# A two-layer graph network: the first adjacency's row sums from TensorE to ScalarE, one cast reordered, one load on another queue

## The chip, the cores and the metric

The kernel runs on one core of one Trainium2 chip. A core has five engines that run side by side, each with its own instruction queue in order: TensorE (PE in the profile, with its weight loads as PEld), VectorE (DVE), ScalarE (ACT), GpSimd (POOL) and SyncE (SP, which issues DMAs here). Sixteen DMA engines move data between DRAM and the on-chip memory. An engine's queue waits at an instruction until the semaphores it needs have been raised by other engines or by DMAs. The metric is device time in microseconds (us) of one whole execution; the time of a kernel is the median of its runs.

## The reference

There are 16 graphs of N = 1024 nodes with C = 128 features. `adj` (16 x 1024 x 1024) holds zeros and ones and is symmetric with a filled diagonal; the kernel's exact path relies on its entries being short numbers. Cut to what matters:

```python
# layer 0: four rounds of a gated network, all graphs apart
h = relu(layernorm(x))
for i in range(4):
    hw = einsum('bnc,cd->bnd', h, weight[i])
    m  = einsum('bjn,bjd->bnd', adj, hw)
    h  = gru_cell(m, h, w_ih[i], w_hh[i], b_ih[i], b_hh[i])
x = x + h * mask
# layer 1: four convolutions, normed over all graphs after each
h = relu(layernorm(x))
for i in range(4):
    h = relu(einsum('bnm,bmc->bnc', adj, h @ W[i]) + b[i])
    mu, var = mean and variance of h over graphs and nodes
    h = gamma[i] * (h - mu) * rsqrt(var + 1e-5) + beta[i]
return x + h
```

## The kernel before

Each product with an adjacency is done in two parts. The left factor is split into a high part, rounded to a format that TensorE multiplies fast (`hw[0]`, a cast on ACT), and the low rest (`hw[1]`, a subtraction on DVE), and both are multiplied with the adjacency's rows (`aggregate_rows`, L520 to L530, 32 matmuls of 128x512 per graph and round). The first part of the kernel runs the gated network, the second the four convolutions.

**The gated network** runs as two streams, `sa` with the even graphs and `sb` with the odd ones. A step (`half_step`, L1105) does the gates of one stream (24 matmuls at L1000, and sigmoids, a tanh and elementwise work on ACT and DVE) and then the sums with the adjacency of the other (L524), while ACT and DVE finish the gates. After a sum ACT copies its two halves out of the accumulators (`m`, L961), and the next step's gates read them. A number `clock[0]` counts the steps: the first two streams' first rounds are steps 3 and 4, step 5 has its gates at 79 us in the trace and a step takes some 17.6 us. In this part the order of every engine is the order of the program text (`manual_schedule` with all five engines, L1170). Work that belongs to no stream's own round is put into a step by `at(step, place, what)`; `due(place)` emits it, and the places of a step are, in order, "ins", "start", "beside0", "looks", "mid", "beside1", "outs", "gap" and "end".

Around the change, this is in the steps:

- `next_load` (L808, "beside0") loads the x of the stream's next graph into one of four buffers of the tag "x" (`flat`, L389). It is issued from ACT's queue. `next_sums` (L811, "gap" of the same step) takes its layer-norm sums on DVE (L664), `next_factors` (L814, "gap" of the next step) the root on ACT (L668) and two small DVE operations. There are 14 such loads, in pairs in neighbouring steps, one pair in eight steps.
- The norm of the layer's output is spread over steps in the same way (`plan`, L825): `store_xmid` (L752, "mid", a DMA from POOL), `blocks` (L680, ACT), `store_ymid` (L755, "mid", from POOL).
- "mid" is emitted by `mids` (L1098): POOL first copies one column of the stream's new h (`pace`, L1101), and so waits for DVE's last operation on it (L1044), then stores.
- The transposer (`transposes`, L618) casts each adjacency row to bf16 on POOL (L615) into one of two buffers `half`, has SP issue a transposing DMA, and at last stores the turned adjacency `adjT_d` for the convolutions.
- In the fourth round of a stream SP loads the next graph's adjacency rows into `stage`, POOL rounds them into `row` tiles (L577), and ACT or DVE looks whether their low bits are zero (`glance`, L580 to L586, an ACTIVATE with an accumulated sum and an output `junk` that nobody reads; `look`, L606, on DVE).

For the first two graphs the rows are in place from the start: `sa.rows` are graph 0's eight tiles of 128x1024, read by the sums of graph 0's four rounds (the last three in steps 3, 5 and 7) and by the transposer, and overwritten with graph 2's from step 8 on.

**The convolutions.** `load_adjT` (L1318) loads eight rows of the turned adjacency in bf16 (`packed`, `block`) and casts them (`wide`, ACT for every third, DVE for the rest) into twelve `row` buffers. In the first convolution the weights are applied after the sums (`first_weights`, L1389); `first_split` (L1381) loads the stored y on POOL's queue, casts it to the high part `chw` on ACT (L1385) and subtracts on DVE (L1386). A `chw` tile shares its buffer with the gated network's `ghw` of the same parity, so the cast can run only after the last matmul that reads that `ghw`. Graph 0 also gets `row_sums` (L1417): 16 matmuls with a tile of ones (`ones_r`, cast at L1463) add up graph 0's rows into two accumulators (`pt_deg`), so that every partition holds every node's row sum, and two ACT copies (L1426) put them into `degree`, which lies in the first 1024 columns of the gated network's `w_mT`. `raw_weights` (L1406) reads `degree` in convolutions 1 to 3, where graph 0's sum is taken before the norm's shift is known and the shift times the row sum is added afterwards (L1413).

The last gates of `sb` (b = 15), the turns of the last h's (`pt_x`, L735) and `last_tail` (L757) overlap with the first convolution. In this part only PE, POOL and SP keep the program's order, and only within the block at L1298 to L1303; a planner with modelled times orders the rest. `tc.issue_after(ins)` is a constraint for it: an instruction of the block that runs on the engine of `ins` comes after `ins` in that engine's queue. `last_m` (L961) is a stream's latest copy of a sum; after the gated network `sb.last_m` is that of graph 15's last round.

Of the kernel before, what the change touches and what calls it, by code (L numbers as in the profile page):

```python
# [8 lines left out]
F32 = mybir.dt.float32  # L9
F32R = mybir.dt.float32r  # L10
BF16 = mybir.dt.bfloat16
U16 = mybir.dt.uint16
I32 = mybir.dt.int32
AF = mybir.ActivationFunctionType
ALU = mybir.AluOpType
AX = mybir.AxisListType
P = 128
HALF = 512
# [323 lines left out]
def exact_path(  # L342
# [21 lines left out]
    nc = tc.nc  # L364
    B, N, C = x.shape
    L = g_weight.shape[0]
    NB = N // P
    NH = N // HALF
# [3 lines left out]
    const = ctx.enter_context(tc.tile_pool(name="const", bufs=1))  # L372
    small = ctx.enter_context(tc.tile_pool(name="small", bufs=2))
    dram = ctx.enter_context(tc.tile_pool(name="dram", bufs=1, space=bass.MemoryType.DRAM))
# [7 lines left out]
    def tmp(name):  # L382
        return ps_t.tile([P, HALF], F32, tag="tmp", name=name)

    adjT_d = [dram.tile([NB, P, N], BF16, tag=f"adjT{b}", name=f"adjT_d{b}") for b in range(B)]
    xmid_d = [dram.tile([N, C], F32, tag=f"xmid{b}", name=f"xmid_d{b}") for b in range(B)]
    ymid_d = [dram.tile([P, N], F32, tag=f"ymid{b}", name=f"ymid_d{b}") for b in range(B)]

    def flat(name):  # L389
        return keep.tile([P, NB, C], F32, tag="x", name=name, bufs=4)  # L390
# [10 lines left out]
    def hw_tiles(b, name):  # L401
        return [keep.tile([P, N], F32R, tag=f"hw{b % 2}{s}", name=f"{name}_{s}") for s in range(2)]
# [5 lines left out]
    nc.vector.memset(eps_t, EPS)  # L408
    ones = const.tile([P, 1], F32, tag="ones", name="ones")
    nc.vector.memset(ones, 1.0)  # L410
    low = const.tile([P, (B + 2) * NB], F32, tag="low", name="low")
    nc.vector.memset(low, 0.0)

# [52 lines left out]
    def turn_hh(i):  # L466

        pt = tmp(f"pt_whh{i}")
        for g in range(3):
            nc.tensor.transpose(pt[:, g * P : (g + 1) * P], wns["hh", i][:, g, :], ident)  # L470
        nc.scalar.copy(w_hhT[:, i, :], pt[:, : 3 * P])

    def turn_ih(prep, w_g, i):

        pt = tmp(f"pt_wih{i}")
        for g in range(3):
            nc.tensor.transpose(pt[:, g * P : (g + 1) * P], wns["ih", i][:, g, :], ident)
        nc.tensor.transpose(pt[:, 3 * P :], w_g[:, i, :], ident)
        both = prep.tile([P, 4 * C], F32, tag="w_both", name=f"w_both{i}", bufs=1)
        nc.scalar.copy(both, pt)  # L480
        turned[i] = both[:, 3 * C :], both[:, : 3 * C]

    def join_layer(i):
        w_gT, w_ihT = turned[i]
        pw = tmp(f"pt_wm{i}")
        nc.tensor.matmul(pw[:, : 3 * P], w_gT, w_ihT, start=True, stop=True)
        nc.scalar.copy(w_mT[:, i, :], pw[:, : 3 * P])
# [29 lines left out]
    def aggregate(pm, hw, rows, g):  # L517
        aggregate_rows(pm, hw, rows, range(g * BH, (g + 1) * BH))
# [14 lines left out]
    with ExitStack() as st:  # L533
        work = st.enter_context(tc.tile_pool(name="work", bufs=2))
        rawd = st.enter_context(tc.tile_pool(name="rawd", bufs=2, space=bass.MemoryType.DRAM))

        def load_x(b, eng):
            xt = flat(f"x{b}")
            eng.dma_start(xt, x[b].rearrange("(k p) c -> p k c", p=P))
            return xt  # L540
# [39 lines left out]
        def glance(b, stage, js):  # L580

            junk = work.tile([P, N], BF16, tag="junk", name=f"junk{b}_{js[0]}", bufs=1)
            for j in js:
                lows = stage[j % 4].bitcast(U16).rearrange("p (n t) -> p n t", t=2)[:, :, 0]
                k = b * NB + j
                nc.scalar.activation(junk, lows, AF.Copy, accum_out=low[:, k : k + 1])  # L586

        def exchange_out(t, name, d=None):
            if d is None:
                d = rawd.tile([P, HALF], F32, tag="cross", name=f"cross_{name}", bufs=8)  # L590
            nc.sync.dma_start(d, t)
            return d
# [25 lines left out]
        def transposes(batches):  # L618

            for b, rows in batches:  # L620
                adjT = turned_tile(f"adjT{b}")
                ahead = transpose_rows(b, rows[0], 0, adjT)
                for j in range(NB):
                    go = ahead
                    if j + 1 < NB:
                        ahead = transpose_rows(b, rows[j + 1], j + 1, adjT)
                    go()
                    yield j
                nc.gpsimd.dma_start(adjT_d[b].rearrange("k p n -> p k n"), adjT)
                yield NB  # L630
# [139 lines left out]
        class Stream:  # L770
# [35 lines left out]
                norm_blocks(self.xt, self.y, self.norm, ks)  # L806

            def next_load(self):  # L808
                self.next_x = load_x(self.b + 2, nc.scalar)

            def next_sums(self):  # L811
                self.next_norm = norm_stats(self.next_x, f"in{self.b + 2}")
# [256 lines left out]
        def at(n, place, go):  # L1069
            agenda.setdefault((n, place), []).append(go)  # L1070
# [5 lines left out]
        def first_step(one, two, gated, halfway):  # L1076

            feed.next_step()
            if one is sa:
                feed.jobs = transposes([(s.b, s.rows) for s in (sa, sb)])  # L1080
            one.split_step()
            feed.some(2)
            two.gate_step(0)
            two.half_away(0)
            if feed.full or (clock[0], "mid") in agenda:
                mids(two)
            feed.some(1)
            two.gate_step(1)
            two.half_away(1)
            gated()  # L1090
            one.agg_step(0)
            halfway()
            feed.some(NB if one is sa else 1)
            one.agg_step(1)
            two.finish()
            clock[0] += 1

        def mids(two):  # L1098

            pace = small.tile([P, 1], F32, tag="pace", name=f"pace{clock[0]}")  # L1100
            nc.gpsimd.tensor_copy(pace, two.new[:, :1])  # L1101
            feed.store()
            due("mid")
# [63 lines left out]
        sa, sb = Stream(0), Stream(1)  # L1167
        every = {getattr(mybir.EngineType, e) for e in ("PE", "DVE", "Activation", "Pool", "SP")}
        prep = st.enter_context(tc.tile_pool(name="prep", bufs=1))
        with tc.manual_schedule(engines=every):  # L1170
# [111 lines left out]
            def ahead(i):  # L1282
                join_layer(i)
                if i + 1 < L:
                    turn_hh(i + 1)

            sa.plan(0)
            sb.plan(1)
            first_step(sa, sb, looks, lambda: ahead(1))
            first_step(sb, sa, lambda: turn_ih(prep, w_g, 2), lambda: ahead(2))  # L1290
            written[0] = False
# [23 lines left out]
    work = ctx.enter_context(tc.tile_pool(name="work2", bufs=2))  # L1315
# [53 lines left out]
    def banks(b, i):  # L1369
        return [acc(t, f"pc{b}_{i}_{t}") for t in (("m0", "m1") if b % 2 == 0 else ("g_r", "g_z"))]  # L1370

    def conv_done(b, i, pm, stats, halfway=None):
        for hf in range(NH):
            dst = feat[b][:, hf * HALF : (hf + 1) * HALF]
            last = nc.scalar.activation(dst, pm[hf], AF.Relu, bias=cvec(0, i))  # L1375
            nc.vector.bn_stats(stats[:, b * NH + hf, :], dst)  # L1376
            if halfway and hf == 0:
                sums = halfway()
        return sums if halfway else last

    def first_split(b):  # L1381
        yt = flat(f"y{b}").rearrange("p k c -> p (k c)")
        nc.gpsimd.dma_start(yt, ymid_d[b])
        hw = hw_tiles(b, f"chw{b}_0")
        nc.scalar.copy(hw[0], yt)  # L1385
        nc.vector.tensor_sub(hw[1], yt, hw[0].bitcast(F32))  # L1386
        return hw

# [17 lines left out]
    def raw_weights(i, pm, aff, stats):  # L1406
# [6 lines left out]
            nc.vector.scalar_tensor_tensor(mt[:, cols], degree[:, cols], aff[1], mt[:, cols], ALU.mult, ALU.add)  # L1413
            nc.tensor.matmul(pc[hf], w_c[:, i, :], mt[:, cols], start=True, stop=True)
        conv_done(0, i, pc, stats)

    def row_sums(rows):  # L1417

        pd = [tmp(f"pt_deg{hf}") for hf in range(NH)]
        for j in range(NB):  # L1420
            for hf in range(NH):
                nc.tensor.matmul(
                    pd[hf], ones_r, rows[j][:, hf * HALF : (hf + 1) * HALF], start=(j == 0), stop=(j == NB - 1)
                )
        for hf in range(NH):
            nc.scalar.copy(degree[:, hf * HALF : (hf + 1) * HALF], pd[hf])  # L1426

    xo = []

# [29 lines left out]
            for n0, n in pieces(k):  # L1459
                nc.gpsimd.dma_start(xo_piece(k, n0, n), by_node(xmid_d[k], n0, n))  # L1460

    ones_r = work.tile([P, P], F32R, tag="ones_r", name="ones_r", bufs=1)
    nc.vector.tensor_copy(ones_r, ones.to_broadcast([P, P]))  # L1463
    degree = w_mT.rearrange("p l c -> p (l c)")[:, :N]

    stats = small.tile([P, B * NH, 6], F32, tag="bn_st", name="stats0")
    hw, waiting = first_split(0), None
    for b in range(B):
        rows = load_adjT(b, 0)
        hw_next = first_split(b + 1) if b + 1 < B else None  # L1470
        pm = banks(b, 0)
        aggregate(pm, hw, rows, 0)
        if waiting:
            last = first_weights(*waiting, stats)
            if b == 1:
                with tc.issue_after(last.ins):
                    sb.rest()
        if b == B - 1:
            hw_next = raw_split(1)
        aggregate(pm, hw, rows, 1)  # L1480
        if b == 0:
            row_sums(rows)
        hw, waiting = hw_next, (b, pm)


# [1 line left out]
    for i in range(1, L):  # L1487
        rows, pm0, hw0 = load_adjT(0, i), banks(0, i), hw
# [6 lines left out]
        hw = conv_hw(1, i, conv_input(1, i, aff, 2))  # L1495
        aggregate_rows(pm0, hw0, rows, range(6, NB))
        for b in range(1, B):
            rows = load_adjT(b, i)
# [18 lines left out]
            hw = hw_next  # L1517
# [9 lines left out]
    for b in range(B):  # L1527
# [3 lines left out]
        for n0, n in pieces(b):  # L1531
# [5 lines left out]
            tag = turns[count % len(turns)]  # L1537
# [60 lines left out]
```

## Time and profile before

| | |
|---|---|
| time, median of 3 runs | 1770.71 us |
| the three runs | 1769.65, 1772.32, 1770.71 us |
| the profiled execution | 1769.17 us |
| span of its instructions | 1767.4 us |
| granted TensorE clock | 0.999 |

| engine | busy us | instructions |
|---|---|---|
| PE | 1752.3 | 6734 |
| DVE | 1289.3 | 2310 |
| ACT | 1112.0 | 1713 |
| POOL | 362.9 | 401 |

| stretch us | PE busy us | DVE | ACT | POOL | DMA share |
|---|---|---|---|---|---|
| 60 to 1110, gated network | 1049.86 | 809.06 | 626.28 | 312.63 | 0.71 |
| 1110 to 1136, its last rounds | 25.70 | 17.61 | 12.52 | 1.10 | 0.92 |
| 1136 to 1156, last gates | 20.00 | 16.48 | 11.05 | 3.62 | 0.68 |
| 1156 to 1169, row sums of graph 0 in it | 12.98 | 9.01 | 10.83 | 1.45 | 0.86 |
| 1169 to 1290, rest of the first convolution | 121.00 | 78.19 | 86.49 | 12.30 | 0.85 |
| 1290 to 1436, the second | 145.66 | 94.74 | 105.16 | 0.00 | 0.65 |

A line of a timeline is: start (us from the span's start), duration, engine, line of the kernel, operation, what it writes <- what it reads, shape, how many in a row; in brackets the idle time of the engine before it and what ended that. "ACTq" is ACT's queue issuing a DMA. Names are the program's with numbers left out. A busy PE can still be slow, since matmuls overlap and their ends are modelled; so starts are compared. The profiled execution is one run, and the difference between its own time and its span lies around the instructions.

### The profile page before, as it was taken

The page shows a single profiled execution, that of the slowest core. Times are in us where ns is not written, and L with a number is a line of the kernel's source. Part 1 is how long each engine was busy: PE and PEld are TensorE (multiplying, and loading weights), DVE is VectorE, ACT ScalarE, POOL GpSimd, SP SyncE. Part 2 cuts the span into 40 slices and gives each one's busy share as a digit, 9 for nine tenths or more (in the row PEclk, how much of TensorE's full clock was granted, in tenths as well). Part 3 has the DMA queues.
Part 4 walks back from the last instruction along what each step waited for, and adds up shares of the span by engine and source line. Part 5 has one row for each costly group of instructions (what it writes and reads, how often), then busy time and mean ns, then how long its engine had stood idle before and what let it go on. Part 6 is the DMA issues. An engine that isn't in the chain of part 4 may idle for free. (4 is left out here: it accounts for less than half of the span.)

```text
span 1767.4 us, 22310 instructions
## 1 busy us (share of the span) xinstructions
PE 1752.3 (99%) x6734; PEld 1192.7 (67%) x6734; DVE 1289.3 (73%) x2310; ACT 1112.0 (63%) x1713; POOL 362.9 (21%) x401
## 2 busy tenths in 40 slices
PE   9999999999999999999999999999999999999997
PEld 5565656565656565656565656577778888888886
DVE  7677877877877887877887786766666666666665
ACT  5356556557556556655655664487677767767765
POOL 4214213322332331321422323110100000000011
PEclk9999999999999999999999999999999999999999
DMA  7458568577686676776866857887866665757667
GB/s 261 138 169 280 166 180 301 158 223 248 196 214 221 221 212 216 238 197 200 270 185 178 305 137 228 287 290 289 292 220 215 234 243 210 256 202 258 230 220 270
DMA packets 376160, 400.14 MB, mean 226 GB/s; under 512 B 158188, under 2 KB 254224, under 8 KB 376032
## 3 DMA queue, kind: packets, MB, share of 16 engines
q1 hardware_dynamic: 342736, 323.59, 58.0%
q0 software_dynamic: 18208, 67.46, 10.2%
q10 hardware_dynamic: 15088, 7.60, 1.5%
q8 instruction: 54, 0.88, 0.2%
q14 instruction: 74, 0.61, 0.1%
HBM read 267.47 MB, written 97.52 MB: 207 GB/s over the span
## 5 line engine op out<-in xcount | busy, mean ns | idle before, releaser
L524 PE MATMUL pm<-row,ghw 128*128 128x512 f32 x2048 | 503.9, 403 | 0.5 <-POOL row L563 0.3
L524 PEld LDWEIGHTS pm<-row,ghw 128*128 128x128 f32 x2048 | 383.6, 188 | 107.1 <-issue 25.6
L524 PE MATMUL pc_m<-wide,chw 128*128 128x512 f32 x1024 | 245.2, 395 | 0.0
L615 POOL CAST half<-row 128x1024 bf16<-128x1024 f32 x128 | 143.7, 1133 | 402.3 <-DMA adjT<-half 387.4
L524 PEld LDWEIGHTS pc_m<-wide,chw 128*128 128x128 f32 x1024 | 190.4, 188 | 41.9 <-issue 3.8
L961 ACT COPY m<-pm 128x512 f32<-128x512 f32 x128 | 68.7, 588 | 195.4 <-PE pm L524 195.4
L1023 ACT ACTIVATE r<-r,vecs 128x512 f32<-128x512 f32 x128 | 92.2, 721 | 152.8 <-DVE r L1020 148.8
L524 PE MATMUL pc_g_r<-wide,chw 128*128 128x512 f32 x464 | 186.9, 403 | 0.3 <-ACT chw L501 0.3
L1019 DVE SCALAR_TENSOR_TENSOR r<-g_hn,vecs,r 128x512 f32<-128x512 f32 x128 | 93.3, 729 | 128.5 <-ACT r L1018 76.3
L524 PE MATMUL pc_g_z<-wide,chw 128*128 128x512 f32 x464 | 181.0, 390 | 0.0
L577 POOL CAST row<-stage 128x1024 fp32r<-128x1024 f32 x112 | 128.1, 1151 | 207.4 <-DMA stage<-in_adj_dram 198.7
L1328 DVE CAST wide<-block 128x1024 fp32r<-128x1024 bf16 x160 | 110.0, 692 | 73.7 <-PE pc_m L524 36.6
L1328 DVE CAST wide<-packed 128x1024 fp32r<-128x1024 bf16 x160 | 110.1, 691 | 71.8 <-PE pc_g_z L524 53.7
L1326 ACT CAST wide<-packed 128x1024 fp32r<-128x1024 bf16 x96 | 100.7, 1049 | 58.5 <-PE pc_m L524 30.3
L1326 ACT CAST wide<-block 128x1024 fp32r<-128x1024 bf16 x96 | 100.6, 1049 | 53.8 <-PE pc_g_z L524 27.7
L1000 PE MATMUL g_r<-m,w_mT 128*128 128x512 f32 x256 | 130.8, 592 | 0.3 <-ACT m L961 0.3
L1000 PE MATMUL g_z<-m,w_mT 128*128 128x512 f32 x256 | 130.7, 592 | 0.0
L1000 PE MATMUL g_xn<-m,w_mT 128*128 128x512 f32 x256 | 130.7, 592 | 0.0
L1018 ACT ACTIVATE r<-g_r,brz 128x512 f32<-128x512 f32 x128 | 87.9, 686 | 53.9 <-PE g_r L1000 53.4
L1376 DVE BATCH_NORM_STATS2 stats<-feat 128x6 f32<-128x512 f32 x128 | 84.1, 686 | 47.0 <-ACT feat L1375 45.9
L1036 DVE TENSOR_TENSOR h<-h,r 128x512 f32<-128x512 f32 x96 | 78.9, 821 | 54.1 <-ACT r L1023 53.9
L1040 DVE TENSOR_TENSOR h<-h,z 128x512 f32<-128x512 f32 x128 | 105.3, 822 | 14.1 <-ACT z L1027 2.1
(185 smaller groups left out, 2810.8 us busy)
## 6 DMA issues: line engine op xcount, KB each, us to landing
block<-adjT_d SPq DMA_DIRECT2D x256, 256.0 KB, 4.7
packed<-adjT_d SPq DMA_DIRECT2D x256, 256.0 KB, 5.7
stage<-in_adj_dram SPq DMA_DIRECT2D x120, 512.0 KB, 5.4
adjT_d<-adjT POOLq DMA_DIRECT2D x16, 2048.0 KB, 7.8
cross_h<-t_h SPq DMA_DIRECT2D x92, 256.0 KB, 2.1
n_h<-cross_h SPq DMA_DIRECT2D x368, 64.0 KB, 2.0
xmid_d<-x POOLq DMA_DIRECT2D x16, 512.0 KB, 6.7
y<-ymid_d POOLq DMA_DIRECT2D x16, 512.0 KB, 5.2
```

The lines of the kernel that those rows point to most:

```text
L524: nc.tensor.matmul(pm[hf], hw[s][:, j * P : (j + 1) * P], rows[j][:, hf * HALF : (hf + 1) * HALF], start=(j == 0 and s == 0), stop=(j == N ...
L577: nc.gpsimd.tensor_copy(t, stage[j % 4])
L615: nc.gpsimd.tensor_copy(t, row.bitcast(F32))
L1000: nc.tensor.matmul(po, wT[:, i, g * C : (g + 1) * C], rhs, start=start, stop=stop)
L1018: nc.scalar.activation(r, pr, AF.Sigmoid, bias=brz[:, 3 * i : 3 * i + 1])
L1019: nc.vector.scalar_tensor_tensor(r, phn, b_hn(i), r, ALU.add, ALU.mult)
L1023: nc.scalar.activation(self.r, self.r, AF.Tanh, bias=b_in(self.i))
L1036: nc.vector.tensor_sub(ho, hin, self.r)
L1040: nc.vector.tensor_mul(ho, ho, self.z)
L1326: nc.scalar.copy(r, t)
L1328: nc.vector.tensor_copy(r, t)
L1376: nc.vector.bn_stats(stats[:, b * NH + hf, :], dst)
```

## The change

Four things change.

1. `row_sums` with its 16 matmuls, two copies and the tile of ones is gone from the first convolution. In its place ACT sums graph 0's rows during steps 5 to 8 of the gated network: eight ACTIVATEs (Copy, f32 128x1024 in, `junk` out) each with an accumulated sum per partition, into one column of `by_row`. The adjacency is symmetric in the reference's inputs, and a row's sum is what `degree` holds for its node.
2. In step 9, place "mid", POOL stores `by_row` as 1024 numbers in DRAM (`degree_d`); with that, `mids` is called in step 9 too. In the first convolution, after graph 2, POOL loads it back into `degree` on all 128 partitions.
3. `next_load` issues x from POOL's queue instead of ACT's.
4. The high part's cast in `first_split` is held behind `sb.last_m` on ACT.

```diff
--- before.py
+++ after.py
@@ -382,6 +382,7 @@
     def tmp(name):
         return ps_t.tile([P, HALF], F32, tag="tmp", name=name)
 
+    degree_d = dram.tile([N], F32, tag="degree", name="degree_d")
     adjT_d = [dram.tile([NB, P, N], BF16, tag=f"adjT{b}", name=f"adjT_d{b}") for b in range(B)]
     xmid_d = [dram.tile([N, C], F32, tag=f"xmid{b}", name=f"xmid_d{b}") for b in range(B)]
     ymid_d = [dram.tile([P, N], F32, tag=f"ymid{b}", name=f"ymid_d{b}") for b in range(B)]
@@ -408,6 +409,7 @@
     nc.vector.memset(eps_t, EPS)
     ones = const.tile([P, 1], F32, tag="ones", name="ones")
     nc.vector.memset(ones, 1.0)
+    by_row = const.tile([P, NB], F32, tag="by_row", name="by_row")
     low = const.tile([P, (B + 2) * NB], F32, tag="low", name="low")
     nc.vector.memset(low, 0.0)
 
@@ -584,6 +586,12 @@
                 lows = stage[j % 4].bitcast(U16).rearrange("p (n t) -> p n t", t=2)[:, :, 0]
                 k = b * NB + j
                 nc.scalar.activation(junk, lows, AF.Copy, accum_out=low[:, k : k + 1])
+
+        def row_sums(rows, js):
+
+            for j in js:
+                junk = work.tile([P, N], BF16, tag="junk", name=f"summed{j}", bufs=1)
+                nc.scalar.activation(junk, rows[j].bitcast(F32), AF.Copy, accum_out=by_row[:, j : j + 1])
 
         def exchange_out(t, name, d=None):
             if d is None:
@@ -806,7 +814,7 @@
                 norm_blocks(self.xt, self.y, self.norm, ks)
 
             def next_load(self):
-                self.next_x = load_x(self.b + 2, nc.scalar)
+                self.next_x = load_x(self.b + 2, nc.gpsimd)
 
             def next_sums(self):
                 self.next_norm = norm_stats(self.next_x, f"in{self.b + 2}")
@@ -1286,6 +1294,16 @@
 
             sa.plan(0)
             sb.plan(1)
+            for n, place, js in (
+                (5, "beside1", (0,)),
+                (6, "beside0", (1,)),
+                (6, "beside1", (2,)),
+                (6, "gap", (3,)),
+                (7, "gap", (4, 5, 6)),
+                (8, "start", (7,)),
+            ):
+                at(n, place, lambda js=js: row_sums(sa.rows, js))
+            at(9, "mid", lambda: nc.gpsimd.dma_start(degree_d.rearrange("(j p) -> p j", p=P), by_row))
             first_step(sa, sb, looks, lambda: ahead(1))
             first_step(sb, sa, lambda: turn_ih(prep, w_g, 2), lambda: ahead(2))
             written[0] = False
@@ -1382,7 +1400,8 @@
         yt = flat(f"y{b}").rearrange("p k c -> p (k c)")
         nc.gpsimd.dma_start(yt, ymid_d[b])
         hw = hw_tiles(b, f"chw{b}_0")
-        nc.scalar.copy(hw[0], yt)
+        with tc.issue_after(sb.last_m.ins):
+            nc.scalar.copy(hw[0], yt)
         nc.vector.tensor_sub(hw[1], yt, hw[0].bitcast(F32))
         return hw
 
@@ -1413,17 +1432,6 @@
             nc.vector.scalar_tensor_tensor(mt[:, cols], degree[:, cols], aff[1], mt[:, cols], ALU.mult, ALU.add)
             nc.tensor.matmul(pc[hf], w_c[:, i, :], mt[:, cols], start=True, stop=True)
         conv_done(0, i, pc, stats)
-
-    def row_sums(rows):
-
-        pd = [tmp(f"pt_deg{hf}") for hf in range(NH)]
-        for j in range(NB):
-            for hf in range(NH):
-                nc.tensor.matmul(
-                    pd[hf], ones_r, rows[j][:, hf * HALF : (hf + 1) * HALF], start=(j == 0), stop=(j == NB - 1)
-                )
-        for hf in range(NH):
-            nc.scalar.copy(degree[:, hf * HALF : (hf + 1) * HALF], pd[hf])
 
     xo = []
 
@@ -1459,8 +1467,6 @@
             for n0, n in pieces(k):
                 nc.gpsimd.dma_start(xo_piece(k, n0, n), by_node(xmid_d[k], n0, n))
 
-    ones_r = work.tile([P, P], F32R, tag="ones_r", name="ones_r", bufs=1)
-    nc.vector.tensor_copy(ones_r, ones.to_broadcast([P, P]))
     degree = w_mT.rearrange("p l c -> p (l c)")[:, :N]
 
     stats = small.tile([P, B * NH, 6], F32, tag="bn_st", name="stats0")
@@ -1478,8 +1484,8 @@
         if b == B - 1:
             hw_next = raw_split(1)
         aggregate(pm, hw, rows, 1)
-        if b == 0:
-            row_sums(rows)
+        if b == 2:
+            nc.gpsimd.dma_start(degree, degree_d.partition_broadcast(P))
         hw, waiting = hw_next, (b, pm)
```

## The prediction

> **What bounds the kernel now.** I read the page first, for the engine that is full.
>
> ```profile
> span 1767.4 us, 22310 instructions
> PE 1752.3 (99%) x6734; PEld 1192.7 (67%) x6734; DVE 1289.3 (73%) x2310; ACT 1112.0 (63%) x1713; POOL 362.9 (21%) x401
> ```
>
> PE is at 99%, no other engine above 73%. A busy PE is not always a PE at its pace, so next the PE timeline. From 107.95 us on, nearly every GRU step begins its sums 17.57 us after the last one (107.95, 125.52, 143.09, 160.67). Inside a sum one 128x512 matmul starts 0.23 us after another; its 389 ns overlaps the next. So any matmul taken away is worth 0.23 us, and work on another engine costs nothing until PE waits for it. The places where the change touches PE, in the PE timeline:
>
> ```profile
> 1117.77 1.02 PE L1000 MATMUL g_r<-h,w_hhT 128*128 128x512 f32 x2
> 1119.09 1.12 PE L1000 MATMUL g_r<-m,w_mT 128*128 128x512 f32 x2 [0.30 <-ACT m L961]
> ...
> 1147.11 0.60 PE L735 MATMUL pt_x<-ident,h 128*128 128x128 f32 x4
> ...
> 1150.76 0.60 PE L735 MATMUL pt_x<-ident,h 128*128 128x128 f32 x4
> ...
> 1158.37 0.39 PE L524 MATMUL pc_g_r<-wide,chw 128*128 128x512 f32 x1
> 1158.77 3.89 PE L1422 MATMUL pt_deg<-wide,ones_r 128*128 128x512 f32 x16
> 1162.50 0.39 PE L524 MATMUL pc_g_z<-wide,chw 128*128 128x512 f32 x1
> ```
>
> L1422 is the row sums that go. Before them stands a stall: g_r<-m starts 1.32 us after g_r<-h, where elsewhere this takes 0.86. The ACT timeline names it:
>
> ```profile
> 1117.51 1.05 ACT L1385 CAST chw<-y 128x1024 fp32r<-128x1024 f32 x1 [5.77 <-PE pm L524]
> 1118.46 1.07 ACT L961 COPY m<-pm 128x512 f32<-128x512 f32 x2
> ```
>
> The first convolution's high part stands ahead of the copies of the sum that PE wants. Last, the one irregular GRU step. Its sums begin at 793.33, the next at 811.35: 18.01 us, so 0.44 us is lost. ACT in that step:
>
> ```profile
> 785.76 0.69 ACT L1018 ACTIVATE r<-g_r,brz 128x512 f32<-128x512 f32 x1
> 788.52 0.41 ACTq L539 DMA_DIRECT2D x<-in_x_dram  x1
> 789.03 1.65 ACT L680 ACTIVATE y_mid<-x,ms_mid,rs_mid 128x128 f32<-128x128 f32 x4 [2.58 <-DMA cross_h<-t_h]
> ```
>
> The sigmoid ends at 786.45 and the x load is issued only at 788.52; everything behind it on ACT stands. I read the wait as one for the store of xmid (L752, issued at 779.55, 3.6 to 8.8 us to landing over its 16), which frees the buffer. All of that chain is late, and DVE's second low part (L932) ends at 798.07. The 19th matmul, the first to read it, was due at 793.33+4.50 = 797.83 (in a regular sum the second starts after 0.63, each further one after 0.2275).
>
> **1. The row sums leave PE.** Next start after the last matmul ahead of them: 1158.37+0.23 = 1158.60 instead of 1162.50: **-3.90 us**. With them go two ACT copies (L1426, 0.58 us each) and one DVE cast (L1463, 0.29), beside PE, worth 0. What is late next: the sums of batch 1 and the casts of their rows. Over 1150 to 1300 us, DVE's and ACT's casts `wide` waited 49 us for PE and 0.6 for DMA, so the rows are there in time; some casts of batches 1 and 2 can even come earlier, since they waited 1.9 us for L1422, which held batch 0's rows. So I take all of 3.90; below it lies 0, if the rows cannot follow (rival C).
>
> **2. Eight sums on ACT.** The trace has no such operation on f32; nearest is L586, the same ACTIVATE with an accumulator on 128x1024 of 16 bits: 1.06 us and 0.19 for the read, 1.16 from one start to the next. Other ACT reads of 128x1024 f32 (L1385) take 1.05. So 8 x 1.2 = 9.6 us of ACT, in idle places of its timeline but for the last. Row 0 goes into 2.75 us of idle before 90.38, row 1 into 1.82 before 102.48, row 2 into 1.92 before 108.29, row 3 into 4.38 before 115.59, rows 4 to 6 (3.5) into 4.31 before 133.16. Cost 0. A Copy under the Sqrt table needs no table load: the m copies at 115.59 run between the Sqrt at 110.90 and the load at 116.68. Row 7 stands at the start of the step at 133.2, ahead of table load and sigmoid, and makes that chain 1.2 us late. Cover: the sums start at 143.09, and their 3rd and 19th matmul, the first to read the low parts, at 143.95 and 147.59; those ended at 141.54 and 145.75. That leaves 2.4 and 1.8 us, more than 1.2. Cost 0; were a sum twice as long, 0.6. Rows 0 to 7 are rewritten by POOL from 139.9, after all sums.
>
> **3. by_row to DRAM and back.** The store is 1024 runs, as xmid's store (L752, 0.90 us on POOL). It adds a `pace` copy (L1101, 0.19) that waits for DVE's h of 160.0; POOL is rounding until 166.1, so it waits for nothing. Behind it stand POOL's last four rounds of that step, ending at 172.3; their rows are first wanted by the sums at 178.2. Cost 0; cover 6 us. The read back is 512 KB of DMA in one batch of the first convolution (9.02 us at 301 GB/s, so 1.7 us of traffic); w_mT is first read at 1307.9. The casts there wait for PE and not for DMA, so 0; uncovered, 1.7.
>
> **4. x on POOL.** ACT loses 14 issues of 0.41 us: beside PE, worth 0, except the 2.07 us wait at 788.5. Without it that step's chain is some 2 us earlier and the 0.3 us lateness goes: **-0.44 us**. POOL gains 14 issues of 0.90 (L752's shape: 128x8 runs of 512 B). They queue behind the transposer's casts that wait for half buffers: after 231.53 instead of 224.62, after 247.50 instead of 240.64, and so in each pair. Landing 3.6 to 8.8 us after the issue (L752), median 6.7: 238.2, against DVE's norm sums that began at 236.54, took 3.0 and were followed by L1019 at 241.48. So by the median DVE is on time, by 8.8 it is 1.9 us late, against 3.3 us of spare: that step's low parts end at 246.0 and 249.7, and PE's sums from 248.53 read them at 249.4 and 253.0. Behind the issue on POOL stand pace, ymid's store and a cast, 0.9 us later: the cast's transposes are issued 4 us after it. Cost 0.
>
> [...] In the rows, POOL's 16 issues at L752 took 885 to 910 ns, with DVE busy beside many. [...]
>
> **5. The high part behind the sum's copies.** The stall at 1119.09 goes: 1.32-0.86 = **-0.46 us**. But chw0's cast (1.05, ACT) and its subtraction (L1386, 1.23, DVE) leave idle time at 1117 to 1120 and now come after 1137. ACT has room (idle 1137.7 to 1138.7 and 1139.4 to 1142.2). On POOL a y load that waits for that subtraction moves from 1120.10 to some 1142, with xmid's store (1139.03) and the next y load (1140.35) behind it; the y's are wanted by the casts of 1155.39 and 1171.00, so 0. DVE has no room:
>
> ```profile
> 1138.85 1.21 DVE L1386 TENSOR_TENSOR chw<-y,chw 128x1024 fp32r<-128x1024 f32 x1
> ...
> 1143.49 0.69 DVE L1036 TENSOR_TENSOR h<-h,r 128x512 f32<-128x512 f32 x1 [0.20 <-ACT r L1023]
> ...
> 1145.69 0.68 DVE L1044 TENSOR_TENSOR h<-h,r 128x512 f32<-128x512 f32 x1
> ...
> 1149.74 0.68 DVE L1044 TENSOR_TENSOR h<-h,r 128x512 f32<-128x512 f32 x1
> ```
>
> From 1136.57 to 1147 it is idle 0.20 us. Its two L1044 end at 1146.37 and 1150.42, just where PE's turns pt_x (1147.11, 1150.76) pick them up. A second subtraction of 1.23 us can make PE stand for 0 (if the turns are put behind more convolution matmuls) to 1.2 us. I take **+0.6**, the middle, since which it is hangs on the planner's order.
>
> **Sum.** -3.90-0.44-0.46+0.6 = -4.2 us. The profiled execution took 1769.17 (span 1767.4 and 1.8 around it): 1765.0. The runs shown have their median at 1770.71, 1.5 above it; the same 4.2 off gives **1766.5**, which I predict.
>
> **Rivals.**
> A, the forecast: PE stays dense, -3.6 to -4.8 us, 1765.9 to 1767.1. 0.60. For it: the even steps and the waits on PE everywhere.
> B: the tail's DVE is the new bound, with the whole 1.2 us and as much again where the second turn or the first convolution matmuls wait for chw0's low part: -4.8+2.4 = -2.4, 1768.3. For it: DVE's full rows above; against: the planner can shift the turns. 0.18.
> C: the change doesn't give what the removed matmuls promise: PE waits for batch 1's or 2's rows instead, the 3.90 is paid back, -0.9, 1769.8. For it: DMA at 85% over 1169 to 1290; against: the 48 us that casts wait for PE. 0.13.
> D, slower: the x loads on POOL land too late. Place: the sums of the step after each first load of a pair. It decides from 1.9 (gap to L1019) + 3.3 (spare) past 236.54, at 241.7, which is 10.2 us after POOL's issue at 231.5; the row's longest is 8.8. If each of 14 loads stood PE up for 0.8 us it is +11.2-4.8 = +6.4, 1777.1. 0.09.
>
> **Numbers.** This kernel's times tell about 0.2%, 3.5 us, from no change. A is faster: 0.60. B and C are the same: 0.31. D is slower: 0.09. Range: A's lower end 1765.9 less the 1.5 by which single runs differ, 1764.4; up to C and 1 us of spread, 1770.8; only D and what lies beyond is left out.
>
> **What would show it.** Step 1: no pt_deg, and PE at 0.23 us a matmul from batch 0 to batch 2. Step 2: eight junk activations of 1.2 us, steps still 17.57. Step 3: a POOL store near 166 with the sums at 178.2 in place. Step 4: the 18.01 us step at 17.57, and norm sums on DVE starting up to 2 us later. Step 5: 0.86 between the g_r's at 1118, and the start of pt_x against L1044's end. I am wrong if any step exceeds 17.57 by tenths, if the casts in the first convolution wait for DMA, or if PE stands before pt_x or the first pc_m by over 1.2 us.

## The result and the profile after

The changed kernel takes **1780.19 us** (median of five runs, 1777.03 to 1784.19) against 1770.71 (1769.65 to 1772.32): ratio **1.0052**, 95% interval 1.0035 to 1.0070. It is slower, by 9.5 us; the forecast was 1766.5. The profiled execution is the shortest of the five, 1777.03.

The page of the changed kernel, its span, its engines, its DMA queues (packets, MB, share of the 16 engines' time) and, from the list of all DMAs, some issues (the last number is the median from issue to landing). Line numbers are 2 to 18 higher than before.

```profile
span 1775.2 us, 22304 instructions
PE 1751.6 (99%) x6718; PEld 1189.6 (67%) x6718; DVE 1283.5 (72%) x2309; ACT 1120.9 (63%) x1729; POOL 376.1 (21%) x418
...
q1 hardware_dynamic: 342736, 323.59, 61.8%
q0 software_dynamic: 20400, 75.33, 13.1%
...
n_h<-cross_h SPq DMA_DIRECT2D x368, 64.0 KB, 2.4
...
adjT<-half SPq DMA_TRANSPOSE x128, 3.3
```

The same lines of the DMA list before:

```profile
q1 hardware_dynamic: 342736, 323.59, 58.0%
...
n_h<-cross_h SPq DMA_DIRECT2D x368, 64.0 KB, 2.0
...
adjT<-half SPq DMA_TRANSPOSE x128, 2.8
```

PE has 16 matmuls fewer and is busy as long as before. What to see is q1: exactly the packets and bytes of before. The same transfers take 7.0% more of the engines' time (61.8 x 1775.2 against 58.0 x 1767.4), a transpose lands after 3.3 us instead of 2.8, a piece of the exchange (n_h) after 2.4 instead of 2.0. Nothing in the diff touches q1's transposes or its exchange.

The waits of PE in the changed kernel (total, times, longest). Before, the list had 0.3 for pm and 0.6 for g_z, and no g_hn:

```profile
PE g_hn L1008 <- DVE r L1027: 3.7, 4, 1.7
...
PE pm L526 <- DVE ghw L940: 1.1, 2, 0.8
PE pm L526 <- ACT ghw L933: 1.0, 1, 1.0
```

Where the time came: I laid the start of each sum with the adjacency beside that of before. The difference is 0.7 at 51 us, stands through all the steps in which ScalarE sums the rows, and then grows in single steps of the gated network: +1.0 at 248, +2.4 at 670, +0.6 at 688, +1.3 at 811, +1.2 at 952, +2.4 at 1092; then -0.6 at 1128, where the high part was moved, +0.3 before the first convolution, -3.9 where the row sums stood, and nothing more up to PE's last matmuls. Behind the start of these (`pt_o`, 1742.32 before, 1748.15 after) the execution takes 27.01 us instead of 25.06, another 1.95. So the expected gains on PE are there, and some 10 us were lost in steps where the change has at most an x load.

One of these steps in the changed kernel, first POOL's x load, then DVE (gaps in brackets):

```profile
233.79 0.89 POOL L541 DMA_DIRECT2D x<-in_x_dram  x1
```

```profile
242.71 0.30 DVE L672 BATCH_NORM_STATS2 st_in<-x 128x6 f32<-128x128 f32 x1 [3.31 <-DMA x<-in_x_dram]
...
245.89 0.73 DVE L1027 SCALAR_TENSOR_TENSOR r<-g_hn,vecs,r 128x512 f32<-128x512 f32 x1
```

DVE's first norm sum of that step before:

```profile
236.54 0.25 DVE L664 BATCH_NORM_STATS2 st_in<-x 128x6 f32<-128x128 f32 x1
```

PE in the changed kernel:

```profile
245.30 1.02 PE L1008 MATMUL g_r<-m,w_mT 128*128 128x512 f32 x2
246.68 1.13 PE L1008 MATMUL g_hn<-h,w_hhT 128*128 128x512 f32 x2 [0.36 <-DVE r L1027]
```

x lands 8.9 us after its issue, DVE's norm sums start at 242.71 instead of 236.54 before, L1027 behind them is late, and PE, which needs the accumulator that L1027 reads, starts g_hn 1.38 us after g_r instead of 0.86 (244.64 and 245.50 before). This looks like rival D. So the first theory was L: x on POOL's queue is the cause. Its rival was R: the row sums, with what comes with them (store, read back, new tiles), are. The expectations below call R's sums and store "rival S" (the later theory S is another), and chance "rival N".

### The profile page after: what moved, and what is told of

It is laid out like the page before. It is cut to its first block, busy times and chain, and to the rows that moved or that the text cites. A ratio compares the mean times of both kernels' runs of the same rounds, so it can differ in the third digit from the quotient of the medians.

```text
span 1775.2 us, 22304 instructions
## 1 busy us (share of the span) xinstructions
PE 1751.6 (99%) x6718; PEld 1189.6 (67%) x6718; DVE 1283.5 (72%) x2309; ACT 1120.9 (63%) x1729; POOL 376.1 (21%) x418
## 3 DMA queue, kind: packets, MB, share of 16 engines
q1 hardware_dynamic: 342736, 323.59, 61.8%
## 5 line engine op out<-in xcount | busy, mean ns | idle before, releaser
L1027 DVE SCALAR_TENSOR_TENSOR r<-g_hn,vecs,r 128x512 f32<-128x512 f32 x128 | 93.0, 727 | 105.2 <-ACT r L1026 60.2
```

What stands on the lines that cost most here:

```text
L1027: nc.vector.scalar_tensor_tensor(r, phn, b_hn(i), r, ALU.add, ALU.mult)
```

## Experiments: which part

Times are medians; beside the experiments the kernel before had its median between 1770.11 and 1770.87.

**x back on ACT, all else as changed.**

```diff
-                self.next_x = load_x(self.b + 2, nc.gpsimd)
+                self.next_x = load_x(self.b + 2, nc.scalar)
```

> The changed kernel with one thing undone: x is issued on ScalarE's queue again. Theory L (the loss is the x load on GpSimd's queue: it is issued some 7 us later and lands some 9 us after its issue, DVE's norm sums and then L1027 come late and PE stands at g_hn): the GRU steps are 17.57 us again, and what is left is the row sums' 3.9 us and the stall of 0.5 us at the last sum's copies, less 0.3 at the turns of the last h: 4.0 us faster than before, about 1766.7. Rival S (the eight sums on ScalarE or the extra step's store cost it): still about 1776 to 1780. Rival N (the first run of the changed kernel was off by chance, as its 0.7 us at the start and its slow exchange at 1087 us hint): about 1774.

Measured 1774.11, ratio 1.0023 (1.0013 to 1.0032). Six of the 9.5 us are gone, but it still loses, in steps at 266, 372, 653, 934 and 1092 us; PE now waits 3.8 us for ACT's z (L1035). Neither L's 1766.7 nor S's 1776 to 1780 came. 1774 is the number of N, but the other kernels with the 32 bytes speak against chance: 1777.30 in 7 executions and 1781.76 in 6, below.

**The x queue alone, on the kernel before.**

```diff
-                self.next_x = load_x(self.b + 2, nc.scalar)
+                self.next_x = load_x(self.b + 2, nc.gpsimd)
```

> The kernel before with x on GpSimd's queue alone. Theory L: all of the loss and none of the gain, 8 to 14 us slower than before, 1779 to 1785, with L1027's waits on the norm sums as in the changed kernel. Rivals S and N: within 2 us of before.

Measured 1770.89, ratio 1.0000 (0.9992 to 1.0009). The 18.01 us step became 17.57, as predicted, another grew by 0.42. **Theory L falls**: 14 loads from POOL by themselves cost nothing.

**The high part alone, on the kernel before** (`issue_after` in `first_split` and nothing else).

> The kernel before with the first convolution's high part held behind the last sum's copies, alone. From the changed kernel's trace: the stall of 0.46 us at the second but last sum goes, 0.3 us comes back at the turns of the last h: -0.2 us, 1770.5, the same. If the planner puts DVE's second subtraction worse without the row sums' removal: up to +0.8.

Measured 1769.90, ratio 0.9997 (0.9988 to 1.0005): the stall goes (-0.57), the turns lose 0.33, one step 0.40.

**The row sums alone**: the changed kernel with x on ACT and without `issue_after`.

> The kernel before with the row sums on ScalarE (their store and load back on GpSimd with them) alone: x on ScalarE's queue, the high part where it was. Theory L and the sum of the prediction: -3.9 us, 1766.8, and steps of 17.57 us from 79 to 170 us. Rival S: no gain, or a loss of several us that shows in those steps.

Measured 1777.3, ratio 1.0032 (1.0021 to 1.0043). So the loss comes with this part. But its sums run at 89 to 136 us, its store at 168 and its read back at 1121, and the steps that lose most are at 231, 372, 653, 934 and 1075. What does it change there? No instruction. It allocates two tiles: `by_row`, 8 f32 a partition in the pool `const`, and `degree_d`, 4 KB in DRAM, each ahead of others. Looking up the addresses that the two programs give to their tiles: `low`, the weights and every SBUF tile of the pools behind stand 32 bytes higher. The rows went from 100864 = 394 x 256 to 100896, the half tiles from 51712 = 202 x 256 to 51744, adjT from 68096 = 266 x 256 to 68128. In the kernel before, x, half, adjT, hw, row, h, half1, m, r and z all began at multiples of 256; after, none did.

## Experiments: placement

New theory S: the 32 bytes in SBUF slow the DMAs. Rivals: D, the shift in DRAM behind `degree_d`; Q, the added transfers and their order.

**32, 128 and 256 unused bytes, on the kernel before.** The edit is shown for 128 bytes; with 32 bytes the tile has NB = 8 columns, with 256 it has 64:

```diff
+    pad = const.tile([P, 32], F32, tag="by_row", name="by_row")
+    nc.vector.memset(pad, 0.0)
     low = const.tile([P, (B + 2) * NB], F32, tag="low", name="low")
```

> The kernel before with nothing but an unused tile of 32 bytes a partition (8 f32, set to zero once) where the change puts by_row: every SBUF tile allocated behind it stands 32 bytes higher (rows at 100896 in place of 100864 = 394 x 256). No sum moves, no DMA is added. Theory S (placement in SBUF): the 32 bytes alone make the DMAs slower and the steps late, as in the run with the row sums alone (1777.3 with some 2.6 to 3.9 us won back by the removed matmuls): 1779 to 1781 us, with drift at steps of 230, 370, 650, 930 and 1075 us. Theory D (the 4 KB of degree_d move the DRAM buffers behind it) and theory Q (the added store, its read back and the pace copy change the order on the queues): 1770.7, no change.

> The same with 128 bytes in place of 32: the tiles stand 128 above a multiple of 256. Theory S with a boundary of 256 bytes: about as slow as with 32 bytes, 1777 to 1781. Theory S with a boundary of 128 bytes or less: 1770.7. Theories D and Q: 1770.7.

> The same with 256 bytes: the tiles move, but stand at multiples of 256 again. Theory S: 1770.7, no change; if it is 1777 or more, it isn't the boundary but any move of the tiles. Theories D and Q: 1770.7.

Measured: 32 bytes **1781.76** (ratio 1.0063, 1.0051 to 1.0075); 128 bytes **1777.30** (1.0043, 1.0030 to 1.0056); 256 bytes **1770.25** (0.9997, 0.9988 to 1.0006). A tile that nobody reads costs 10.9 us, and eight times its size costs nothing. The 32 bytes lie 0.8 above the range named, with late steps where they were named (231, 372, 653, 934, 1075) and at 793. A lower granted clock isn't the loss: four of the six executions with 32 unused bytes had 0.998, like most of the kernel before, and took 1777.33 to 1783.10. S holds: of the three offsets tried, 32 and 128 cost and 256 doesn't, as with a boundary of 256 bytes. The transfers of the kernel with 32 unused bytes, then with 256:

```profile
q1 hardware_dynamic: 342736, 323.59, 60.7%
...
n_h<-cross_h SPq DMA_DIRECT2D x368, 64.0 KB, 2.4
...
adjT<-half SPq DMA_TRANSPOSE x128, 3.3
```

```profile
q1 hardware_dynamic: 342736, 323.59, 58.2%
...
adjT<-half SPq DMA_TRANSPOSE x128, 3.0
```

With 32 bytes these are the signs of the change. The transposes alone don't tell the placement: in the six kernels here with their tiles at multiples of 256 the median is 2.8 to 3.1. q1's share does: 58.0 to 59.5% there, 60.5 to 61.8% in the five with all tiles moved.

How slower transfers make PE wait is read from one step, in the same program with and without the 32 bytes. POOL and ACT before:

```profile
214.91 0.89 POOL L629 DMA_DIRECT2D adjT_d<-adjT  x1 [1.31 <-DMA adjT<-half]
```

```profile
223.41 0.69 ACT L1018 ACTIVATE r<-g_r,brz 128x512 f32<-128x512 f32 x1
224.62 0.41 ACTq L539 DMA_DIRECT2D x<-in_x_dram  x1
225.08 1.65 ACT L680 ACTIVATE y_mid<-x,ms_mid,rs_mid 128x128 f32<-128x128 f32 x4 [0.98 <-DVE r L1019]
...
227.24 0.67 ACT L1027 ACTIVATE z<-g_z,brz 128x512 f32<-128x512 f32 x1
```

POOL, ACT and PE with 32 unused bytes:

```profile
218.37 0.89 POOL L631 DMA_DIRECT2D adjT_d<-adjT  x1 [3.59 <-DMA adjT<-half]
```

```profile
224.48 0.69 ACT L1020 ACTIVATE r<-g_r,brz 128x512 f32<-128x512 f32 x1
229.11 0.41 ACTq L541 DMA_DIRECT2D x<-in_x_dram  x1
229.57 1.65 ACT L682 ACTIVATE y_mid<-x,ms_mid,rs_mid 128x128 f32<-128x128 f32 x4 [4.40 <-DMA cross_h<-t_h]
231.12 0.71 ACT L1025 ACTIVATE r<-r,vecs 128x512 f32<-128x512 f32 x1
231.73 0.67 ACT L1029 ACTIVATE z<-g_z,brz 128x512 f32<-128x512 f32 x1
```

```profile
229.86 1.02 PE L1002 MATMUL g_xn<-m,w_mT 128*128 128x512 f32 x2
232.45 1.12 PE L1002 MATMUL g_z<-h,w_hhT 128*128 128x512 f32 x2 [1.57 <-ACT z L1029]
```

PE stands 1.1 us behind the kernel before here. The last four transposes took 3.1 to 4.4 us instead of 2.7 to 2.8, so the last one of this graph ends later and the 2 MB store of the turned matrix is issued 3.46 us later: 2.4 us late against PE. It is under way until 226.38 instead of 222.61, and a cross_h issued beside it, which took 3.14 us from 221.38, takes 7.79 from 221.23. That the store is what slows it is my reading. ACT's sigmoid r ends as early in the step as it did, but the x issue behind it now stands until 229.11 instead of 224.62, z follows at 231.73 instead of 227.24, and PE waits. The trace names the landing of cross_h (229.02) as the end of that wait. It isn't the store of xmid, which lands only at 229.34, behind the issue. In the trace's semaphore events the x issue waits for the semaphore that this cross_h raised last and that x's own landing raises next. In the kernel before the same holds for six x issues, each 0.10 us behind the landing of a cross_h. So x waits for a transfer whose data it doesn't use. The x issues in the late steps at 231, 372, 653, 793 and 934 us all leave ACT idle for 3.2 to 3.9 us like this, and PE's wait for z over the whole execution, 0.6 us before, becomes:

```profile
PE g_z L1002 <- ACT z L1029: 6.9, 6, 1.6
```

**The whole change, with by_row cut out of 256 bytes.**

```diff
-    by_row = const.tile([P, NB], F32, tag="by_row", name="by_row")
+    by_row = const.tile([P, 64], F32, tag="by_row", name="by_row")[:, :NB]
```

> The whole change, with by_row cut out of a tile of 256 bytes a partition, so that the tiles behind it stand at multiples of 256 as before; degree_d stays first among the DRAM buffers, its store and read back stay. Theory S: the loss is gone and the gains of the steps stay: -3.90 (row sums), -0.44 (x on GpSimd's queue), -0.57 and +0.33 (high part), together -4.6, so 1766.1, the time first predicted. Theories D and Q: 1780 as the change, since all that they name is still there.

Measured **1766.45** (1765.98 to 1767.97), ratio 0.9978 (0.9969 to 0.9987). This beats both kernels. `degree_d`, the store and the read back are all in it: D and Q fall. Its page and the step of 248 us, DVE and PE:

```profile
span 1764.5 us, 22304 instructions
...
q1 hardware_dynamic: 342736, 323.59, 59.5%
```

```profile
239.41 0.29 DVE L672 BATCH_NORM_STATS2 st_in<-x 128x6 f32<-128x128 f32 x1 [2.22 <-DMA x<-in_x_dram]
...
242.59 0.73 DVE L1027 SCALAR_TENSOR_TENSOR r<-g_hn,vecs,r 128x512 f32<-128x512 f32 x1
```

```profile
246.19 1.02 PE L1008 MATMUL g_hn<-h,w_hhT 128*128 128x512 f32 x2
```

x is late here too (DVE waits 2.22 us for it), but L1027 runs at 242.59, 3.3 us earlier than in the changed kernel, and PE has no gap. Half of the 3.3 us is x's issue (232.24 instead of 233.79; in both POOL waited for a transpose before it), half its way to landing (7.15 us instead of 8.89). q1's share is 59.5%, above the 58.0 of before, without a loss. The steps from 248 us to the last rounds last 17.57 each.

**The row sums alone, with by_row cut out of 256 bytes.**

> The row sums alone (x loads on ScalarE's queue, high part where it was), as in the run that gave 1777.3, but with by_row in a tile of 256 bytes, so that nothing behind it loses its multiple of 256. Theory S: 3.90 off, 1766.6 to 1767.2, and the sums on ScalarE, the store and the read back cost nothing. If those cost anything by themselves, it is seen here, above 1767.2. From the run with x moved alone, x's queue is worth nothing, so this should stand within 1 us of the whole change with the same tile (1766.45).

Measured 1767.64 (ratio 0.9983, 0.9974 to 0.9992), 0.4 above the range named and 1.2 from the whole change, where 1 was named: the same edit as the run with 1777.3, with the tiles at multiples of 256. The -3.9 at the row sums is there, and after 170 us no step is longer than 17.73, but for the one with the high part's stall at 1119, 18.14 as before.

**One group of tiles at a time, on the kernel before,** 32 bytes above a multiple of 256, by pads of 32 and 224 bytes around it: x and half; adjT; all behind adjT. Where x and half move, `low`, the weights and the small tiles, which stand ahead of them, move too.

> The kernel before; only the x tiles and the half tiles (tags x and half: the x loads, both ends of the exchange cross_h and n_h, pair and h's transfers, the packed rows of the convolutions) stand 32 bytes above a multiple of 256, the tile adjT and all behind it at multiples of 256. A theory that the exchange is what suffers (n_h 2.4 us in place of 2.0, and PE's late steps stand where the exchange stands): most of the loss, 1777 to 1781. A theory that the turned matrix suffers (transposes 3.3 us in place of 2.8, 2 MB stores): 1771 to 1773. A theory that it is the engines' own reads and writes of the rows: 1770.8.

> The kernel before; only the tile adjT (target of the transposes, source of the 2 MB store to adjT_d, and in the convolutions the target of the block loads) stands 32 bytes above a multiple of 256. If the exchange is what suffers: 1771 to 1772. If the turned matrix is: transposes at 3.3 us and 1777 to 1781. If the engines' own reads: 1770.8.

> The kernel before; x, half and adjT at multiples of 256, but all behind them (the split hw, the rows, h, half1 that the transposes read, y, m, r, z) 32 bytes above. If the exchange or the turned matrix as a target is what suffers: 1771 to 1772. If the engines' own reads and writes of rows, h, m, r and z are slowed: most of the loss, 1777 to 1781, with longer matmuls or copies in the rows of the profile.

Measured: x and half 1773.90 (ratio 1.0019, 1.0010 to 1.0028), adjT 1771.21 (1.0003, 0.9994 to 1.0012), the rest 1771.93 (1.0009, 1.0000 to 1.0018). The x and half tiles, through which the exchange runs, cost most, but far less than expected; together the three cost 5.1 us, all at once 10.9. Transposes took 3.2 to 3.3 us in all three, even where neither of their tiles was moved, but that is little above the 3.1 of the high part alone, with no tile moved. The engines' own work is hardly longer: with 32 unused bytes ACT is busy for 1111.8 us and DVE for 1282.0, against 1112.0 and 1289.3 before, a matmul of the sums takes 403 ns in both, and POOL is busy for 366.1 us against 362.9; in the changed kernel ACT's copy of a sum (`m`) takes 588 ns as before, and DVE's cast of a turned row 691 against 691 to 692. So it is the transfers that suffer, and not the reads and writes of ACT, DVE and PE.

**Two groups at a time.**

> The kernel before; x, half and all behind adjT 32 bytes above a multiple of 256, adjT alone at a multiple of 256. Moved by themselves the three groups cost 3.3 (x and half), 0.6 (adjT) and 1.3 us (the rest), 5.1 in all, while all three together cost 10.9 to 11.1. If the costs add up and only the intervals are wide: 3.3+1.3 = 4.6, 1775.3. If it is a matter of cover that is used up (each slows the DMAs by its share, and PE only waits for what goes beyond the spare time): more than the sum, 1777 to 1780, with waits at the steps of 231 and 371 us, which no group alone made late.

> The kernel before; x, half and adjT 32 bytes above, all behind adjT at multiples of 256. If the costs add up: 3.3+0.6 = 3.9, 1774.6. If it is used-up cover: more than the sum, 1775 to 1779; the group missing here gave the most engine time of the hardware queue (60.0% in place of 58.0), so this should lose less than the run without adjT.

Measured 1776.01 (1.0034, 1.0022 to 1.0046) and 1776.81 (1.0037, 1.0023 to 1.0050). Both medians lie above the sums (1775.3, 1774.6); beside this batch's 1770.11 the sums are 1774.7 and 1774.0, the first within its run's interval, the second just below it. The first run also misses the 1777 named for used-up cover. It has a late step at 231 us (+2.3), which neither of its groups had alone, but none at 371. This speaks for a common cover that is used up, but the order that I expected of the two (less lost without the rest) didn't come, and the intervals don't settle it. How much each tile's transfers carry, and whether the costs add up, **stays open**.

## Why the prediction was wrong

The gains came, by the steps of the prediction: the sum was -4.2 us, and with the tiles in place it measures -4.4 (1766.45 against 1770.87 in the same batch). That 1766.45 is so near to 1766.5 is partly luck: the terms of step 5 were each off by 0.1 to 0.3, and the 0.44 of step 4 can't be seen in the median of its own run. What failed is a term that the sum did not have. In the rivals, C's -0.9 leaves out the +0.6 of step 5; with it C is -0.3.

1. **Row sums leave PE, -3.90**: right. PE is 3.88 earlier there in the changed kernel, and no cast of the convolution waits long for DMA (0.4 us). Rival C, the rows late, didn't come.
2. **Eight sums on ACT, 0**: right. Each takes 1.05 and 0.19 us, all ran between 89 and 136 us, and the steps there stay even:

```profile
143.75 7.84 PE L526 MATMUL pm<-row,ghw 128*128 128x512 f32 x32
...
161.32 7.84 PE L526 MATMUL pm<-row,ghw 128*128 128x512 f32 x32
...
178.90 3.29 PE L526 MATMUL pm<-row,ghw 128*128 128x512 f32 x12
```

3. **by_row to DRAM and back, "Cost 0": the step that failed.** Its transfers do cost nothing (issued at 168.07 and 1120.9, and the kernel with 256 bytes has them). But the step counted what the new tiles make the queues do, and not where they push the other tiles. The 32 bytes of `by_row`, put at nothing, cost 1780.19 - 1766.45 = 13.7 us in this kernel and 10.9 in the one before. The diff shows the line, its place ahead of `low`, and its size; that tiles' addresses decide anything was in no row of the trace before, since all stood at multiples of 256.
4. **x on POOL, -0.44**: the step of 18.01 us is 17.57 with x alone on POOL, but it is worth nothing measurable in the whole. That x's queue mends that step isn't shown either: with the row sums alone in 256 bytes and x on ACT, ACT stands as long before x (2.58 us) and the step is 17.57 all the same, and so it is with 32 unused bytes. Nor was it a wait for the store of xmid, as the prediction read it: the row shown there names cross_h, which landed 0.10 us before the issue. An issue of 0.90 us from POOL came as the step had it: the 14 took 882 to 900 ns.
5. **High part behind the copies, -0.46 and +0.6**: measured -0.57 and +0.33. PE in the changed kernel, at the stall that went and at the second turn:

```profile
1127.72 1.02 PE L1008 MATMUL g_r<-h,w_hhT 128*128 128x512 f32 x2
1128.59 1.02 PE L1008 MATMUL g_r<-m,w_mT 128*128 128x512 f32 x2
...
1163.43 0.63 PE L743 MATMUL pt_x<-ident,h 128*128 128x128 f32 x4 [0.17 <-DVE h L1052]
```

The g_r's are 0.87 apart again; the turn waits 0.17. Rival B, DVE in the tail, had the right place and a quarter of its price.

**Rival D**, at 0.09, named where a large part of the loss shows: PE late behind norm sums that wait for x. Its point was a landing after 241.7, some 10 us after POOL's issue; x lands at 242.68, 8.9 after an issue that came 2.3 us later than the prediction's 231.5 (0.7 of it lateness from the start; POOL waited for a transpose before it). But its cause isn't the queue alone, as these four medians show:

| | x issued by ACT | x issued by POOL |
|---|---|---|
| tiles at multiples of 256 bytes | 1770.71 (before) | 1770.89 (x alone) |
| tiles 32 bytes above | 1774.11 (x back on ACT) | 1780.19 (the change) |

With the tiles moved, x from POOL costs 6 us more than x from ACT; with the tiles in place it costs nothing. The step of 248 us shows two parts of it, POOL's wait for a slower transpose and x's own longer way; how the 6 us divide over the whole run isn't shown. The upper row has the row sums on TensorE, the lower one on ScalarE and the high part moved, so the table is read along its rows.

## What to carry to other kernels

A new tile is also a shift of all tiles behind it: compare the addresses that the two programs give, and pad a small new tile to the boundary (here 256 bytes: 1766.45 us instead of 1780.19) or put it behind all others (not tried here). A first sign is a queue with the same packets and bytes and more engine time (a rise of 1.5 points also stands in the kernel that won, so it is a sign and no proof); a loss that shows in steps which the diff doesn't touch is looked for in what all steps share. Undoing one part at a time found the part here, but only moving tiles with no other change found the cause in it.

## What the runs showed of the hardware

The time of transfers depended on where in SBUF the tiles begin, by 256 bytes. From q1's share x 16 engines x span / 342736 packets, a packet took 47.9 ns before, 48.0 with 256 unused bytes, 50.1 with 128 and 50.4 with 32. Over all runs it was 47.9 to 49.0 with the tiles at multiples of 256 and 50.1 to 51.2 with all of them moved.

A boundary of 256 bytes agrees with the three offsets tried: 1781.76 us at 32 above, 1777.30 at 128 and 1770.25 at 256. By what mechanism a tile's address makes a packet longer, none of the runs shows. Of the two offsets that cost, 128 was not the worse: 50.1 ns a packet against 50.4 with 32.
